# Chunks of both layers fetched row by row through SyncE, and a second range of layer 2's products placed at the end of layer 1

## The chip, the cores and the metric

The kernel runs on one core of one Trainium2 chip. The metric is the device time of one execution in microseconds (us), median of several runs. Engines are named as the profile names them: PE is TensorE (PEld its weight loads), DVE VectorE, ACT ScalarE, POOL GpSimd, SP SyncE; SPq is SyncE's stream of DMA issues.

## What is computed

Two layers of a graph network over 6250 nodes and 100000 edges, all in float32, then a residual and a layer norm. The edges are sorted by target node, and the targets are squared random numbers, so low nodes have many edges.

```python
def _gin_agg(h, src, dst, eps, n_nodes):
    agg = jax.ops.segment_sum(h[src], dst, num_segments=n_nodes)
    return (1.0 + eps) * h + agg
...
h = _gin_agg(x, src, dst, eps1, n)            # x: 6250 x 256
h = jax.nn.relu(h @ W1a + b1a)                # 256 -> 512
h = jax.nn.relu(h @ W1b + b1b)                # 512 -> 512
h = _gin_agg(h, src, dst, eps2, n)
h = jax.nn.relu(h @ W2a + b2a)                # 512 -> 512
out = h @ W2b + b2b                           # 512 -> 256
...
x = _layernorm(x + out)
```

## The kernel before

Nodes are taken in 49 tiles of 128, edges in 782 chunks of 128. The first 288 chunks belong to the seven lowest tiles, the heavy ones (`HEAVY`). They are not fetched at all: the kernel counts how often each source occurs for each heavy tile, and multiplies the matrix of counts with all node rows. In layer 1 that is `first_products`, over 13 ranges of four tiles (`RANGE`; the last range has one tile). The counts are written to DRAM (`counts`) and read back (`ci`, line 1557) for layer 2, where `second_products` splits each range's rows into two parts (`upper`, `xr`, lines 1532 to 1540) and makes 7 x 4 x 2 products for it (line 1644).

The other 494 chunks stand in 85 groups of 2 to 16 chunks, which are gone through from high nodes to low. For each chunk GpSimd fetches 128 rows by an indirect DMA (`gather`, line 507), from x in layer 1 (1 KB rows) and from h1 in layer 2 (2 KB rows). Four gathers make a piece, six pieces are in flight, in the buffers `early` and, in layer 2 only, `late` too. TensorE sums a chunk by a matmul with a selection matrix (`sums`, line 1172); `merge` moves the sums to their nodes (line 1235) and VectorE adds them to the accumulators (line 1245). When a block of tiles is complete, `dense` turns it over (line 1289), multiplies twice (lines 1342 and 1375) and stores h1, or the layer norm's result. Layer 2 goes first through two groups (`FORES`) that need little of the newest h1.

One chunk of some groups takes another way, in layer 1 only. `ferrying` loads its 128 row numbers into SyncE's registers, 16 at a time, and SyncE issues one transfer per row into `b2b_c`, a buffer that later holds a bias. The last matmul of the group reads `b2b_c` instead of the gather's buffer. Which groups these are is worked out beforehand (`ferries`, from the constants in `FERRY`): a group is chosen if 128 rows can be brought by the time its gathers have landed.

The order of instructions on every engine is fixed when the kernel is built. A planner (`Plan`) plays the whole layer through with assumed costs: processes ask for an engine, a buffer or a point in time, and each instruction is emitted when its request is granted. The assumed pitch of a gather is `GATHERS`, 1.28 us in layer 1 and 1.265 us in layer 2. An assumed time for a load to land (`LOAD`, `SEEDS`, `COUNTS`, `WHOLE`) only sets where the load's reader stands in its engine's order; on the chip the reader waits for the load itself. SyncE's issues cost nothing in the plan. On the chip each engine executes its own list in order and stops at the first instruction whose inputs or buffers are not ready.

`AHEAD2` says how many ranges of layer 2's products are placed in layer 1's order, at the lowest urgency (`first = 6`). Before, it is one: the last range, of one tile.

Of the kernel before, what the change touches and what calls it, by code (L numbers as in the profile page):

```python
# [10 lines left out]
F32 = mybir.dt.float32  # L11
I32 = mybir.dt.int32
# [5 lines left out]
P = 128  # L18
# [3 lines left out]
SLOTS = 32  # L22
# [25 lines left out]
PATIENT = 16.0  # L48
SOWN2 = 25.0
WEIGHT2 = 4.0  # L50
FERRY = (45.0, 14.0, 5.0, 16, 610.0)
LEAD = 1.5
LATE = (6, 8)
HASTE = -20.0
AHEAD2 = 1
ACCS2 = 4
AFTER = 4.0
ZEROS = 7
# [117 lines left out]
GATHERS = (1.28, 1.265)  # L176
# [181 lines left out]
def tile_gin_residual_layernorm(  # L358
# [106 lines left out]
    FORETOLD = range(min(lo[g] for g in FORES), max(hi[g] for g in FORES) + 1)  # L465
    orders = {1: list(reversed(range(BEGIN[0], NG)))}
    orders[2] = FORES + [g for g in reversed(range(BEGIN[1], NG)) if g not in FORES]
    ferries, t, free = [], FIRST, FERRY[0]
    for g in orders[1]:
        n = len(members[g])  # L470
        t += GATHERS[0] * n
        ready = free + FERRY[1] * P / FERRY[3] + FERRY[2]
        if ready <= t + LANDINGS[0] and t < FERRY[4] and members[g][-1][0] < full:
            ferries.append(g)
            t -= GATHERS[0]
            free = t + LANDINGS[0] + FERRY[2]
    pieces = {
        number: [
            (g, chunks[i : i + BURST])
            for g in order  # L480
            for chunks in [members[g][: -1 if number == 1 and g in ferries else None]]
            for i in range(0, len(chunks), BURST)
        ]
        for number, order in orders.items()
# [311 lines left out]
    def ordered(ctx):  # L796
# [42 lines left out]
        def layer(number, pools, table, width, scale, weights, ba, wide, at=None, aside=None, right=None):  # L839
# [299 lines left out]
            def sums():  # L1139
                size = 2 if once else 1  # L1140
                turns = [order[k : k + size] for k in range(0, len(order), size)]
                turn_of = {g: gs for gs in turns for g in gs}
                last = {g: i for i, (g, _) in enumerate(pieces[number])}
                final = next(i for i, (g, _) in enumerate(pieces[number]) if g in turns[-1])
                shared = {}
                i = 0
                while i < len(pieces[number]):
                    n = 1 if i >= final or (not once and pieces[2][i][0] in FORES) else min(
                        JOIN[number - 1], final - i
                    )  # L1150
                    some = range(i, i + n)
                    for i in some:
                        yield ("until", selected[pieces[number][i][0]])
                        yield ("until", arrived[i])
                        if once and i == last[pieces[1][i][0]] and pieces[1][i][0] in ferries:
                            yield ("until", ferried[pieces[1][i][0]])
                    for i in some:
                        gs = turn_of[pieces[number][i][0]]
                        if gs[0] not in shared:
                            shared[gs[0]] = yield ("get", banks, 0)  # L1160
                    yield ("on", "PE", TURN + SUMS * width * n, 0)
                    for i in some:
                        g = pieces[number][i][0]
                        gs = turn_of[g]
                        token = shared[gs[0]]
                        at = gs.index(g) * width
                        pm = bank[token.number][:, at : at + width]
                        sel, _, sel_token, _ = sels[g]
                        rows_, reads = gathered.pop(i)
                        for l, (c, b) in enumerate(pieces[number][i][1]):  # L1170
                            part = [c_ for c_, b_ in members[g] if b_ == b]
                            mm = nc.tensor.matmul(  # L1172
                                pm[b * SLOTS : (b + 1) * SLOTS],
                                sel[:, c - groups[g][0], :], rows_[:, l, :],
                                start=(c == part[0]),
                                stop=(c == part[-1] and (once or g not in FORES)),
                            )
                            if l == 0:
                                together(mm, reads[1:])
                        last_sum[i] = mm  # L1180
                        if once and i == last[g] and g in ferries:
                            c, b = members[g][-1]
                            part = [c_ for c_, b_ in members[g] if b_ == b]
                            nc.tensor.matmul(
                                pm[b * SLOTS : (b + 1) * SLOTS], sel[:, c - groups[g][0], :], b2b_c,
                                start=(c == part[0]), stop=True,
                            )
                            plan.then(landed[g].set)
                        if once:
                            begun_with["last_sum"] = mm  # L1190
                        fetch_rows(i + PIECES)
                        if i == last[g]:
                            sel_token.used()
# [889 lines left out]
            permits = Room(plan, SIDE, False)  # L2083
            if once:
                begun = [Event(plan) for _ in STEPS]
            def ferrying():
                yield ("rest", FERRY[0])
                n = FERRY[3]
                for g in ferries:
                    c = members[g][-1][0]  # L2090
                    for o in range(0, P, n):
                        _, rows_in = nc.values_load_multi_w_load_instructions(
                            src[c * P + o : c * P + o + n].rearrange("(a b) -> a b", a=1),
                            engines=[mybir.EngineType.SP], min_val=0, max_val=N - 1,
                            skip_runtime_bounds_check_because="an edge comes from a node",
                        )
                        for j, v in enumerate(rows_in):
                            nc.sync.dma_start(b2b_c[o + j : o + j + 1, :], x[bass.ds(v, 1), :])
                        yield ("rest", FERRY[1])
                    plan.at(plan.now + FERRY[2], ferried[g].set)  # L2100
                    yield ("until", landed[g])
                nc.sync.dma_start(b2b_c, b2b.partition_broadcast(P))

            ferried = {g: Event(plan) for g in ferries}
            landed = {g: Event(plan) for g in ferries}

            def fetching():
                yield ("rest", WEIGHTS if once else SOWN2 - plan.now)
# [4 lines left out]
                        yield ("rest", WEIGHT2)  # L2113

            plan.start(fetching())
            grouped = [b for b in range(len(blocks)) if any(uses[t] for t in blocks[b])]
            if once:
                for i in range(PIECES):
                    fetch_rows(i)
                plan.start(seeding(grouped, {}))  # L2120
                plan.start(seeding([b for b in range(len(blocks)) if b not in grouped], wanted))
                plan.start(selecting())
                plan.start(counting())
                plan.start(ferrying())
                first_products()
            else:
                second_products(list(reversed(range(len(ranges))))[AHEAD2:])
                begins = [b for b in grouped if blocks[b][0] >= tiles]
                plan.start(seeding([b for b in begins if blocks[b][0] not in FORETOLD], {}))
                plan.start(seeding_late([b for b in begins if blocks[b][0] in FORETOLD]))  # L2130
                for g in FORES:
                    plan.start(late_edges(g))
                plan.start(late_rows())
                plan.start(selecting())
                plan.ending = HASTE
                for i in range(PIECES):
                    fetch_rows(i)
# [37 lines left out]
    def general(ctx):  # L2175
# [8 lines left out]
        w2a_s, w2b_s, b2b_s, fetch = second(after)  # L2184
        for _ in fetch():
            pass
        acc1 = [gdram.tile([ROWS, D], F32, name=f"acc1_{k}") for k in range(NACC)]
        acc2 = [gdram.tile([ROWS, H], F32, name=f"acc2_{k}") for k in range(NACC)]

# [239 lines left out]
```

## Time and profile before

| | us |
|---|---|
| median of 3 runs | 1304.05 (1303.57 to 1305.85) |
| profiled execution, whole | 1301.3 |
| its span, first to last instruction | 1299.5 |
| TensorE busy | 1186.0 |
| GpSimd busy | 954.9 |
| VectorE busy | 877.5 |
| ScalarE busy | 621.5 |

Busy times are those of instructions; an indirect DMA keeps GpSimd busy while it writes the transfer's descriptors, and the 0.30 us between two of them count as idle. SyncE only issues transfers and loads registers, so it has no busy time here. The mean TensorE clock granted was 0.962 of full speed.

### The profile page before, as it was taken

How to read it: one execution, taken by the hardware profiler on the slowest of the kernel's cores; microseconds unless marked ns; L12 is line 12 of the kernel's file. 1: busy time of each engine (PE TensorE's matmuls, PEld its weight loads, DVE VectorE, ACT ScalarE, POOL GpSimd, SP SyncE). 2: the span in 40 equal slices, each digit the busy share in tenths (PEclk: the TensorE clock that was granted, in tenths of full speed). 3: DMA queues.
4: the chain of work that ended last, by engine and by line, in shares of the span. 5: the costliest groups of instructions: out<-in, count | busy, mean ns of one | idle time of the engine just before them, and what ended most of it. 6: DMA issues, size and time to landing. Idle time of an engine off the chain costs nothing.

```text
span 1299.5 us, 20725 instructions
## 1 busy us (share of the span) xinstructions
PE 1186.0 (91%) x6125; PEld 768.3 (59%) x6125; DVE 877.5 (68%) x2085; ACT 621.5 (48%) x1140; POOL 954.9 (73%) x997
## 2 busy tenths in 40 slices
PE   6879888889889989899788999899999999999987
PEld 4445455555455545455445677667776676766667
DVE  7997985878687979832156787678866665644334
ACT  6227766467646654674264453434343444432212
POOL 6777777777777777777777677777777777777770
PEclk9889999999999999899789899899999999999999
DMA  7446666567666665776599998898898899877771
GB/s 219 151 142 211 198 201 203 180 209 226 190 186 208 206 215 163 240 247 204 185 343 340 318 313 257 268 292 279 268 312 274 296 299 301 295 245 236 244 229 39
DMA packets 161978, 306.35 MB, mean 236 GB/s; under 512 B 26137, under 2 KB 94127, under 8 KB 161860
## 3 DMA queue, kind: packets, MB, share of 16 engines
q0 software_dynamic: 63040, 193.79, 47.9%
q1 hardware_dynamic: 77866, 86.72, 20.4%
q10 hardware_dynamic: 20954, 24.45, 5.4%
q8 instruction: 52, 0.85, 0.3%
q14 instruction: 66, 0.54, 0.1%
HBM read 274.42 MB, written 30.44 MB: 235 GB/s over the span
## 4 chain that ended last, share of the span: by engine, by line
PE 48%; DMA 17%; DVE 14%; ACT 8%; issue 6%; POOL 3%; SPq 2%; ACTq 1%; DVEq 1%; POOLq 0%
PE bank L1342 13%; PE bank L1375 10%; PE bank L1644 9%; PE bank L1172 7%; PE bank L1235 4%; DVE at L2074 3%; PE bank L1783 3%; DMA ci<-counts 3%; DMA late<-h,places 2%; DMA acc<-h 2%; DVE acc L1245 2%; DMA counts<-ci 2%; POOL early L507 2%; DVE cb L1857 2%; PE bank L1889 2%
## 5 line engine op out<-in xcount | busy, mean ns | idle before, releaser
L507 POOL DMA_INDIRECT early<-in_x_dram,srcs x490 | 481.5, 983 | 152.8 <-issue 132.0
L507 POOL DMA_INDIRECT early<-h,places x238 | 226.7, 953 | 75.4 <-issue 63.7
L507 POOL DMA_INDIRECT late<-h,places x232 | 221.9, 956 | 72.1 <-issue 57.3
L1245 DVE SCALAR_TENSOR_TENSOR acc<-bank,mask,acc 128x256 f32<-128x256 f32 (+1 forms) x360 | 205.1, 605 | 47.2 <-PE bank L1235 44.3
L1375 PE MATMUL bank<-w1b_s,ht 128*128 128x512 f32 (+1 forms) x392 | 188.8, 608 | 1.4 <-ACT ht L1352 0.8
L1342 PE MATMUL bank<-zt,w2a_s 128*128 128x256 f32 (+2 forms) x736 | 154.8, 364 | 0.2 <-ACT zt L1301 0.2
L1172 PE MATMUL bank<-early,sel 128*32 128x256 f32 (+1 forms) x1480 | 130.8, 468 | 24.1 <-DMA early<-h,places 8.5
L1644 PE MATMUL bank<-upper,cf 128*128 128x512 f32 (+1 forms) x343 | 148.8, 434 | 1.9 <-ACT upper L1532 1.1
L1342 PEld LDWEIGHTS bank<-zt,w2a_s 128*128 128x128 f32 x736 | 131.2, 193 | 24.1 <-issue 4.2
L1644 PE MATMUL bank<-xr,cf 128*128 128x512 f32 (+1 forms) x343 | 137.4, 401 | 1.1 <-DVE xr L1537 1.1
L2074 DVE TENSOR_TENSOR at<-bank,at 128x490 f32 x174 | 115.8, 666 | 28.3 <-ACT cf L1731 16.4
L1235 PE MATMUL bank<-split,to 128*128 128x256 f32 (+3 forms) x340 | 104.1, 426 | 18.8 <-DVE split L1226 6.9
L1026 DVE TENSOR_TENSOR sel<-iota,slot 128x256 f32<-128x256 f32 (+2 forms) x116 | 50.7, 437 | 98.4 <-PE bank L1172 95.0
L1375 PEld LDWEIGHTS bank<-w1b_s,ht 128*128 128x128 f32 (+1 forms) x392 | 74.2, 193 | 72.0 <-issue 60.7
L1342 PE MATMUL bank<-zt,w1a_s 128*128 128x256 f32 (+2 forms) x432 | 106.1, 397 | 9.4 <-ACT ht L1352 5.4
L1571 ACT CAST cf<-ci 128x512 fp32r<-128x512 uint16 (+1 forms) x91 | 54.1, 595 | 125.6 <-PE bank L1644 103.3
L1783 PE MATMUL bank<-xh,cf 128*128 128x512 f32 (+1 forms) x343 | 103.6, 438 | 9.3 <-DVE xh L1710 9.2
L1889 PE MATMUL bank<-cb,ca 128*128 128x490 f16 x288 | 86.0, 389 | 19.9 <-DVE at L2074 8.2
L1342 PEld LDWEIGHTS bank<-zt,w1a_s 128*128 128x128 f32 x432 | 84.2, 214 | 33.4 <-ACT ht L1352 6.3
L1172 PEld LDWEIGHTS bank<-early,sel 128*32 128x32 f32 x1480 | 40.2, 111 | 106.6 <-issue 62.5
L1710 DVE TENSOR_TENSOR xh<-bank,xh 128x512 fp32r<-128x512 f32 (+1 forms) x100 | 66.8, 672 | 43.1 <-ACT bank L1708 43.0
L1857 DVE TENSOR_SCALAR cb<-numbers,spot 128x490 f16<-128x490 f16 x288 | 90.7, 356 | 6.6 <-PE bank L1889 6.4
(193 smaller groups left out, 1764.0 us busy)
## 6 DMA issues: line engine op xcount, KB each, us to landing
raw<-in_x_dram SPq DMA_DIRECT2D x48, 512.0 KB
h<-h1r ACTq DMA_DIRECT2D x48, 256.0 KB
xr<-h SPq DMA_DIRECT2D x11, 1024.0 KB
counts<-ci ACTq DMA_DIRECT2D x84, 128.0 KB
ci<-counts SPq DMA_DIRECT2D x84, 128.0 KB
acc<-h SPq DMA_DIRECT2D x18, 512.0 KB
b2b_c<-in_x_dram SPq DMA_DIRECT2D x512, 1.0 KB
early<-in_x_dram,srcs POOLq DMA_INDIRECT x490
```

Source lines behind the costliest of these rows:

```text
L507: nc.gpsimd.indirect_dma_start(out=rows_[:, j, :], out_offset=None, in_=table, in_offset=bass.IndirectOffsetOnAxis(ap=rows_in[:, c - first ...
L1172: mm = nc.tensor.matmul(pm[b * SLOTS : (b + 1) * SLOTS], sel[:, c - groups[g][0], :], rows_[:, l, :], start=(c == part[0]), stop=(c == par ...
L1235: nc.tensor.matmul(pu[:, i * width : (i + 1) * width], to[:used], split[:used, l, :], start=(once or l == 0), stop=(once or l == 1),)
L1245: nc.vector.scalar_tensor_tensor(acc[t], pu[:, i * width : (i + 1) * width], mask[:, t - lo[g], g : g + 1], acc[t], op0=ALU.mult, op1=ALU.add,
L1342: nc.tensor.matmul(ph[:, (f - o) * TILES * P : (f - o) * TILES * P + nb], wa[:, k, f * P : (f + 1) * P], zt[:, k, :nb], start=(k == 0), st ...
L1375: nc.tensor.matmul(po[:m], ht[:, f, i * P : i * P + m], wb[:, f, :], start=(f == 0), stop=(f == KH - 1),)
L1644: nc.tensor.matmul(bank[token.number][:, :width], cf[:m, j, :], of[:m, j, :], start=(j == 0 and of is upper), stop=(j == len(ks) - 1 and o ...
L1710: begun_with["halves"] = nc.vector.tensor_tensor(xh[:m, two, 1, :], ap, xh[:m, two, 0, :], op=ALU.subtract)
L1783: nc.tensor.matmul(bank[tokens[i].number][:, : 2 * width], cf[:m, j, :], xh[:m, j, :, :].rearrange("p a d -> p (a d)"), start=(k == 0), st ...
L1857: made = nc.vector.tensor_scalar(token.tile, numbers, spot[:, c : c + 1], None, op0=ALU.is_equal)
L1889: mm = nc.tensor.matmul(bank[token.number][:, : NT * W], a.tile[:, c % BATCH, :], b.tile, start=(j == 0), stop=(j == n - 1),)
L2074: nc.vector.tensor_tensor(to, bank[token[0].number][:, : NT * W].rearrange("p (k w) -> p k w", w=W), to, op=ALU.add,)
```

## The change

More chunks take the row-by-row way, in both layers. In layer 1 batches hold 32 rows instead of 16. In layer 2 two buffers alternate: the first 512 columns of `srcs` and `dstf`, which layer 2 does not need any more; the row numbers are first written to a small table in DRAM (`rows2`). Both buffers are saved to DRAM at the end of layer 1 and restored in `general`, the branch for inputs that the main path can't handle. `AHEAD2` goes from 1 to 2, so that range 11 (four tiles) follows the last range in layer 1's order.

```diff
-FERRY = (45.0, 14.0, 5.0, 16, 610.0)
+FERRY = 32, 20.0, 5.0
+FERRY_FROM = (40.0, 5.0)
+FERRY_TO = (612.0, 596.0)
...
-AHEAD2 = 1
+AHEAD2 = 2
...
-    ferries, t, free = [], FIRST, FERRY[0]
-    for g in orders[1]:
-        n = len(members[g])
-        t += GATHERS[0] * n
-        ready = free + FERRY[1] * P / FERRY[3] + FERRY[2]
-        if ready <= t + LANDINGS[0] and t < FERRY[4] and members[g][-1][0] < full:
-            ferries.append(g)
-            t -= GATHERS[0]
-            free = t + LANDINGS[0] + FERRY[2]
+    ferries = {}
+    for number, order in orders.items():
+        ferries[number], free = [], [FERRY_FROM[number - 1]] * number
+        t, until = (FIRST, HASTE)[number - 1], FERRY_FROM[number - 1]
+        for g in order:
+            t += GATHERS[number - 1] * len(members[g])
+            ready = max(until, free[0]) + FERRY[1] * P / FERRY[0]
+            if (
+                ready + FERRY[2] <= t + LANDINGS[number - 1] and t < FERRY_TO[number - 1]
+                and members[g][-1][0] < full and not (number == 2 and g in FORES)
+            ):
+                ferries[number].append(g)
+                t -= GATHERS[number - 1]
+                until = ready
+                free = free[1:] + [t + LANDINGS[number - 1] + FERRY[2]]
+    rows2 = dram.tile([len(ferries[2]), P], I32, name="rows2")
+    lent = [
+        (t[:, :H], dram.tile([P, H], t.dtype, name=f"lent{i}")) for i, t in enumerate((srcs, dstf))
+    ]
...
-                        if once and i == last[pieces[1][i][0]] and pieces[1][i][0] in ferries:
-                            yield ("until", ferried[pieces[1][i][0]])
+                        if i == last[pieces[number][i][0]] and pieces[number][i][0] in ferried:
+                            yield ("until", ferried[pieces[number][i][0]])
...
-                                pm[b * SLOTS : (b + 1) * SLOTS], sel[:, c - groups[g][0], :], b2b_c,
+                                pm[b * SLOTS : (b + 1) * SLOTS], sel[:, c - groups[g][0], :], by_row[g],
...
+            by_row = [b2b_c] if once else [t.bitcast(F32) for t, _ in lent]
+            by_row = {g: by_row[i % len(by_row)] for i, g in enumerate(ferries[number])}
...
             def ferrying():
-                yield ("rest", FERRY[0])
-                n = FERRY[3]
-                for g in ferries:
-                    c = members[g][-1][0]
+                n = FERRY[0]
+                if not once:
+                    for i, g in enumerate(ferries[2]):
+                        c = members[g][-1][0] - NC2
+                        nc.sync.dma_start(
+                            rows2[i : i + 1, :].rearrange("a b -> b a"), places2[:, c : c + 1]
+                        )
+                yield ("rest", FERRY_FROM[number - 1] - plan.now)
+                for i, g in enumerate(ferries[number]):
+                    if i >= number:
+                        yield ("until", landed[ferries[number][i - number]])
+                    c = members[g][-1][0] * P
+                    listed = src[c : c + P].rearrange("(a b) -> a b", a=1) if once else rows2[i : i + 1, :]
                     for o in range(0, P, n):
                         _, rows_in = nc.values_load_multi_w_load_instructions(
-                            src[c * P + o : c * P + o + n].rearrange("(a b) -> a b", a=1),
-                            engines=[mybir.EngineType.SP], min_val=0, max_val=N - 1,
+                            listed[:, o : o + n], engines=[mybir.EngineType.SP],
+                            min_val=0, max_val=N - 1 if once else N,
...
                         for j, v in enumerate(rows_in):
-                            nc.sync.dma_start(b2b_c[o + j : o + j + 1, :], x[bass.ds(v, 1), :])
+                            nc.sync.dma_start(
+                                by_row[g][o + j : o + j + 1, :], table[bass.ds(v, 1), :]
+                            )
                         yield ("rest", FERRY[1])
                     plan.at(plan.now + FERRY[2], ferried[g].set)
-                    yield ("until", landed[g])
-                nc.sync.dma_start(b2b_c, b2b.partition_broadcast(P))
+                if once:
+                    yield ("until", landed[ferries[1][-1]])
+                    nc.sync.dma_start(b2b_c, b2b.partition_broadcast(P))
+                    for t, keeps in lent:
+                        yield ("rest", 8.0)
+                        nc.sync.dma_start(keeps, t)
```

## Rows read from the trace of the kernel before

**Rows 1.** Timeline of GpSimd: start, duration, instruction, idle before it and its releaser

```profile
636.13 0.94 POOL L507 DMA_INDIRECT early<-in_x_dram,srcs  x1 [0.30 <-issue]
638.39 0.94 POOL L507 DMA_INDIRECT early<-h,fore  x1 [1.32 <-issue]
...
1263.40 0.95 POOL L507 DMA_INDIRECT late<-h,places  x1 [0.30 <-DMA late<-h,places]
```

**Rows 2.** Gathers by tile: count, durations in ns, first and last start

```profile
L507 POOL DMA_INDIRECT early<-in_x_dram,srcs x490: 942/946/1614, 6.5 to 636.1; - x164
L507 POOL DMA_INDIRECT early<-h,places x238: 940/946/1211, 668.6 to 1258.4; - x119
...
L507 POOL DMA_INDIRECT late<-h,places x232: 942/946/1227, 681.2 to 1263.4; - x116
```

**Rows 3.** Waits of GpSimd from 640 to 1270 us: total, times, longest

```profile
POOL late L507 <- PE bank L1172: 3.2, 6, 1.7
POOL early L507 <- PE bank L1172: 3.2, 1, 3.2
```

**Rows 4.** Stretches: length, busy PE, PEld, DVE, ACT, POOL; clock, DMA share, GB/s

```profile
700.00:750.00 50.00, 43.41 (x220) 30.32 (x219) 35.00 (x60) 23.29 (x43) 35.84 (x38) 0.93 0.96 329
900.00:1000.00 100.00, 99.80 (x542) 71.47 (x541) 73.33 (x145) 43.68 (x80) 75.69 (x80) 1.00 0.88 289
```

**Rows 5.** Timeline of TensorE: sums that waited for gathers, and the end

```profile
639.09 1.08 PE L1172 MATMUL bank<-early,sel 128*32 128x256 f32 x8 [4.45 <-DMA early<-in_x_dram,srcs]
...
1253.55 1.30 PE L1172 MATMUL bank<-early,sel 128*32 128x512 f32 x8 [4.42 <-DMA early<-h,places]
...
1271.08 1.06 PE L1172 MATMUL bank<-late,sel 128*32 128x512 f32 x8
...
1290.73 1.89 PE L1375 MATMUL bank<-w2b_s,ht 128*128 128x256 f32 x8
```

**Rows 6.** SyncE's instructions of a row (L2098) and of a batch (L2092)

```profile
L2098 SPq FUSED_REGOPS  x512: 37/37/47, 19.4 to 532.7; - x171
L2098 SPq MOVE b2b_c<-in_x_dram x512: 29/29/38, 19.5 to 532.8; - x171
L2098 SPq DMA_DIRECT2D b2b_c<-in_x_dram x512: 224/228/309, 19.6 to 532.9; - x171
...
L2092 SPq TENSOR_LOAD <-in_src_dram_ptr x32: 1021/1936/3752, 15.6 to 520.4; - x32
...
L2092 SPq TENSOR_LOAD <-in_src_dram x32: 1724/1972/3207, 17.2 to 523.7; - x32
```

**Rows 7.** Timeline of SyncE's issues where the layers meet

```profile
595.72 3.69 SPq L1557 DMA_DIRECT2D ci<-counts  x2
640.25 0.93 SPq L1460 DMA_DIRECT2D xr<-h  x2
```

**Rows 8.** Waits of ScalarE, 40 to 560 us (two rows), 665 to 1260 us (one)

```profile
ACT xh L1701 <- DMA raw<-in_x_dram: 19.3, 6, 5.4
...
ACT acc L1002 <- DMA acc<-in_x_dram: 16.4, 5, 7.1
...
ACT acc L1002 <- DMA acc<-h: 17.2, 6, 5.9
```

**Rows 9.** Timelines of ScalarE and TensorE around one late seed

```profile
818.80 1.15 ACT L1002 ACTIVATE acc<-acc,e 128x1024 f32<-128x1024 f32 x1 [3.68 <-DMA acc<-h]
...
821.72 1.12 PE L1289 MATMUL bank<-ident,acc 128*128 128x128 f32 x4 [3.31 <-DVE xr L1537]
```

**Rows 10.** Timeline of TensorE: two products of layer 2 in a run

```profile
1207.82 0.39 PE L1644 MATMUL bank<-xr,cf 128*128 128x512 f32 x1
1208.05 0.39 PE L1644 MATMUL bank<-upper,cf 128*128 128x512 f32 x1
```

**Rows 11.** DMA queue of SyncE: packets, MB, share; whole span, then 130.3 to 147.3 us

```profile
q1 hardware_dynamic: 77866, 86.72, 20.4%
...
q1 hardware_dynamic: 79, 0.05, 1.0%
```

More of the change, by code (lines that the diff above doesn't have):

```diff
@@ L480, in tile_gin_residual_layernorm @@
             for g in order
-            for chunks in [members[g][: -1 if number == 1 and g in ferries else None]]
+            for chunks in [members[g][: -1 if g in ferries[number] else None]]
             for i in range(0, len(chunks), BURST)
@@ L1180, in sums @@
                         last_sum[i] = mm
-                        if once and i == last[g] and g in ferries:
+                        if i == last[g] and g in ferried:
                             c, b = members[g][-1]
@@ L2085, in layer @@
                 begun = [Event(plan) for _ in STEPS]
+            ferried = {g: Event(plan) for g in ferries[number]}
+            landed = {g: Event(plan) for g in ferries[number]}
+            by_row = [b2b_c] if once else [t.bitcast(F32) for t, _ in lent]
+            by_row = {g: by_row[i % len(by_row)] for i, g in enumerate(ferries[number])}
             def ferrying():
-                yield ("rest", FERRY[0])
-                n = FERRY[3]
-                for g in ferries:
-                    c = members[g][-1][0]
+                n = FERRY[0]
[11 more added lines that the diff above has]
+                    listed = src[c : c + P].rearrange("(a b) -> a b", a=1) if once else rows2[i : i + 1, :]
                     for o in range(0, P, n):
                         _, rows_in = nc.values_load_multi_w_load_instructions(
-                            src[c * P + o : c * P + o + n].rearrange("(a b) -> a b", a=1),
-                            engines=[mybir.EngineType.SP], min_val=0, max_val=N - 1,
+                            listed[:, o : o + n], engines=[mybir.EngineType.SP],
+                            min_val=0, max_val=N - 1 if once else N,
                             skip_runtime_bounds_check_because="an edge comes from a node",
@@ L2097, in ferrying @@
                         for j, v in enumerate(rows_in):
-                            nc.sync.dma_start(b2b_c[o + j : o + j + 1, :], x[bass.ds(v, 1), :])
+                            nc.sync.dma_start(
+                                by_row[g][o + j : o + j + 1, :], table[bass.ds(v, 1), :]
+                            )
                         yield ("rest", FERRY[1])
                     plan.at(plan.now + FERRY[2], ferried[g].set)
-                    yield ("until", landed[g])
-                nc.sync.dma_start(b2b_c, b2b.partition_broadcast(P))
-            ferried = {g: Event(plan) for g in ferries}
-            landed = {g: Event(plan) for g in ferries}
+                if once:
[4 more added lines that the diff above has]
+                        nc.sync.dma_start(keeps, t)
             def fetching():
@@ L2115, in layer @@
             plan.start(fetching())
+            plan.start(ferrying())
             grouped = [b for b in range(len(blocks)) if any(uses[t] for t in blocks[b])]
@@ L2123, in layer @@
                 plan.start(counting())
-                plan.start(ferrying())
                 first_products()
@@ L2186, in general @@
             pass
+        for t, keeps in lent:
+            nc.sync.dma_start(t, keeps)
         acc1 = [gdram.tile([ROWS, D], F32, name=f"acc1_{k}") for k in range(NACC)]
```

## Prediction

> **What bounds the kernel now.** I read the profile in this order: GpSimd's timeline, the gathers counted by tile, GpSimd's waits, the stretches by engine, TensorE's timeline where the layers meet and where the kernel ends, then SyncE's part.
>
> GpSimd's timeline comes first because it hardly has a hole. A gather is followed by the next one 1.25 us later (0.95 us of work, 0.30 us of issue), and from the last gather of layer 1 at 636.13 us to the first of layer 2 at 638.39 us little less than one gather is lost; the last starts at 1263.40 us [rows 1]. The gathers by tile give the counts: 490 in layer 1, 238 and 232 of layer 2 through the two buffers, and 12 more into each buffer for the two groups that go first [rows 2]. So layer 1's 490 take 6.5 to 637 us, 1.29 us each, and layer 2's 494 take 638.4 to 1264.4 us, 1.27 us each. The reader is to see that layer 2's run is paced by GpSimd itself: over its whole stretch it waits for the buffer's reader on TensorE for only 6.4 us [rows 3].
>
> Yet TensorE is nearly as full. From 900 to 1000 us it is busy 99.80 of 100 us; only from 700 to 750 us, where the DMA engines are 0.96 busy, does it have 6.6 us free [rows 4]. It stands still for want of a gather at two notable places: 4.45 us before layer 1's last sum and 4.42 us at 1253.55 us [rows 5]. After the last sum at 1271.08 us it has 21.5 us of work to 1292.6 us, and 6.9 us of closing steps follow it [rows 5]. So two clocks run side by side: GpSimd's count of gathers, and TensorE's work plus its stalls. Whichever is slower sets the end, and a gain on one counts only as far as the other can follow.
>
> The sum is made against the profiled execution: 1301.3 us, of which 1299.5 us are span. It lies 2.75 us under the median of 1304.05 us; I apply the change in span to the median.
>
> **The change: chunks brought row by row.** How many there are follows from the planner's lines. Before, a chunk takes 8 batches of 16 rows at 14 us plus 5 us, and the next one waits until the buffer has been used; ready times are 162, 283, 405 and 532 us: four chunks, which is the 512 row transfers of the trace [rows 6]. After, a chunk takes 4 batches of 32 rows at 20 us, from 40 us on: ready at 120, 210, 301, 392, 483 and 574 us, so six. In layer 2 two buffers alternate, so a chunk becomes ready every 80 us, from 85 to 565 us of the layer's own clock: seven. GpSimd therefore makes 9 gathers fewer, 2 in layer 1 and 7 in layer 2. At the pitch of 1.25 us that is 11.3 us; at the means of 1.29 and 1.27 us, 11.5 us. I take 11.3 us, because the excess over 1.25 us is not tied to single gathers. TensorE's share does not fall: each chunk still needs its product, only the source changes.
>
> **What SyncE pays.** A row costs 37 + 29 + 228 ns = 0.294 us of SyncE, and a batch two register loads of 1.94 and 1.97 us before it [rows 6]. A batch of 16 holds the queue for 8.6 us, one of 32 for 13.3 us, out of 20 us that the planner gives it. In layer 1 this is 24 batches, 319 us, in place of 32 batches, 275 us; in layer 2 it is new: 28 batches, 372 us. The copies of the row numbers out to DRAM (7 small transfers), the saving of two buffers and the load of the bias all lie near the layer's border, where SyncE has nothing to issue from 599.4 to 640.25 us [rows 7]; I cost them at nothing. Without that gap they would cost SyncE some ten issues of 0.3 to 0.5 us. The trace shows no transfer of 4-byte pieces out of a tile; from below it is nothing, from above the whole gap of 41 us could not be filled by seven.
>
> What is queued behind a batch matters more. SyncE issues in order, so a load of seeds (acc), of x (raw), of a range (xr) or of counts (ci) waits up to 13.3 us behind one, and ScalarE then waits for its landing, in order too. Layer 1 shows the price with batches of 8.6 us: ScalarE waits 19.3 us for raw and 16.4 us for acc. In layer 2, without batches, it waits 17.2 us for acc [rows 8]. Scaled by 13.3/8.6 = 1.55, layer 1's 35.7 us become 55, or 20 more; layer 2's acc waits, if they go to layer 1's 16.4 x 1.55 = 25, grow by 8. That is 28 us more on ScalarE, an estimate.
>
> How much reaches TensorE? One event can be followed: ScalarE waits 3.68 us for acc and TensorE 3.31 us three us later [rows 9], a share of 0.9. Of the 17.2 us in all, though, I find no second stop of that kind in the middle of layer 2, where TensorE is full [rows 4]; 3.31 of 17.2 is 0.19. The bounds are thus 28 x 0.19 = 5 us and 28 x 0.9 = 25 us of new stalls. I take 5 us, because TensorE usually has products queued that need none of this.
>
> **The second range.** 7 x 4 x 2 = 56 products of layer 2 move ahead of its start. In a run one begins 0.23 us after the other [rows 10], so 12.9 us of TensorE's work leave layer 2 and go to the end of layer 1. This is a move, not a saving: it pays as far as it fills time in which TensorE waits for gathers there, 4.45 us in the largest gap [rows 5]. ScalarE converts 7 counts and splits 4 tiles more in the same stretch, and SyncE loads the range (1 MB) and 0.9 MB of counts there rather than after 640 us. Taking 1.9 MB out of a stretch that moves 329 GB/s is up to 5.8 us of DMA time, and TensorE has 6.6 us of idling there [rows 4] that this could shorten. Bounds 0 and 5.8 us; I take 3 us. If the products come late instead, they stay in layer 2 at no loss against before.
>
> **Sum.** GpSimd's clock: -11.3 us. TensorE's clock: the two waits for gathers go, -4.45 - 4.42 = -8.9; the border, -3; new stalls, +5; together -6.9 us. The slower clock decides: about -7 us, so 1304.05 - 7 = 1297 us.
>
> **Rivals.**
> *GpSimd alone decides.* If the new stalls hide wholly and the border gives all of its 5.8 us, TensorE's clock moves by up to -14.7 us and the gathers decide: -11.3 us, 1293 us. For it: GpSimd has almost no waits on TensorE. Against it: TensorE has almost no slack. Were a fifth of the 21.5 us behind the last sum done earlier as well, it would be 1289 us.
>
> *SyncE's batches starve ScalarE* (the other side). The place is the loads of acc, raw and xr behind a 13.3 us batch; the price at a share of 0.9 is 25 us: -8.9 - 3 + 25 = +13 us, 1317 us. It turns slower when the stalls pass 11.9 us, a share of 0.43. For it: the followed event. Against it: batches of 8.6 us already hold SyncE for some 60% of layer 1 (8.6 of 14 us by the planner), and gathers keep their pace there.
>
> *The move is no gain.* If the products do not fit before layer 1's last tiles, and the stalls eat what is left, -8.9 + 8 leaves about -1 us, 1303 us. For it: the counts must be written out and read back before each product. Against it: by the code six of the seven tiles' counts come from earlier passes, and layer 1 makes this range's rows among its first.
>
> *One DMA engine takes all rows.* A stretch with 32 row transfers shows 79 packets on SyncE's queue, so a row is at most two packets and cannot be spread over 16 engines. The whole queue took 20.4% of 16 x 1299.5 us for 86.72 MB, 48.9 us per MB [rows 11]. Seven chunks of 128 rows of 2 KB are 1.84 MB, 90 us. Spread evenly this is 0.01 of the engines over the 560 us. On a single engine it is 0.16 on top of 0.88 [rows 4], so 1.04; the excess of 22 us would make gathers late by as much, and -11.3 + 22 gives +11 us, 1315 us. No row shows which engine moves a row. The Trainium skill speaks for this one (DMA: Bandwidth & Descriptors, section "Why a DMA increments its semaphore by 16 and not by 1"): a transfer from SyncE runs on a number of engines that divides its slowest dimension, and those are the lowest-numbered ones; by that rule a transfer on one engine always meets the same one. Layer 1's rows are half as long, at a lower load, so the gathers' even pace there neither confirms nor refutes it.
>
> **Chances.** The forecast 0.48 (its own range 1291 to 1301 us), GpSimd alone 0.20, the move is no gain 0.12, SyncE's batches 0.16, one engine 0.04. A change under 0.2%, 2.6 us, cannot be told from none here. Faster: 0.20 and all but 0.03 of the forecast, 0.65. Same: 0.12 + 0.03 = 0.15. Slower: 0.16 + 0.04 = 0.20. The range of 1289 to 1310 us takes in the full gain with the shorter end, and the batches' case up to half way to its full price; beyond it lie the rest of that case and the single engine.
>
> **What would show it.** Right: 488 gathers in layer 1 and 487 in layer 2; the pitch still 1.25 us; layer 1's last gather near 633.6 us and layer 2's last 7 to 11 us earlier; products of the second range between 600 and 660 us; ScalarE's waits for raw and acc near 55 and 25 us. Wrong: waits of TensorE for the row buffers; GpSimd waiting for TensorE by more than some 10 us; TensorE's idle time in layer 2 above 10 us per 100 us; waits for gathers that land later than before. If row transfers start behind waits on SyncE, the matmul of a brought chunk stops TensorE, which I cost at nothing since rows are due 5 us and more ahead of their use.

## The result, and the profile after

The change makes the kernel slower: 1645.3 us (1641.35 to 1650.02) in place of 1304.05, a ratio of 1.2615 with a 95% interval of 1.258 to 1.2651. The forecast was 1297 us with a range up to 1310. Ratios compare the fast runs of two kernels alone (those within 1.5% of a kernel's fastest), so that a ratio can differ a little from that of the medians.

The profiled execution took 1644.9 us, of which 1643.2 us are span: 343.7 us more than before. First the page of the changed kernel: busy time by engine (part 1), and the chain of work that ended last, by engine and by line (part 4).

```profile
PE 1245.9 (76%) x6125; PEld 801.3 (49%) x6125; DVE 876.6 (53%) x2085; ACT 619.0 (38%) x1140; POOL 942.5 (57%) x988
...
PE 37%; DMA 18%; SPq 18%; issue 9%; DVE 8%; ACT 7%; POOL 1%; ACTq 1%; DVEq 0%; POOLq 0%
SPq L2124 13%; PE bank L1387 9%; PE bank L1354 9%; PE bank L1184 5%; PE bank L1656 5%; SPq L2118 4%; DMA acc<-h 4%; DMA raw<-in_x_dram 3%; PE bank L1247 3%; PE bank L1795 3%; DVE acc L1257 2%; DMA sown<-h 2%; DMA acc<-in_x_dram 2%; PE bank L1901 1%; POOL early L519 1%
```

The same line of the kernel before:

```profile
PE 48%; DMA 17%; DVE 14%; ACT 8%; issue 6%; POOL 3%; SPq 2%; ACTq 1%; DVEq 1%; POOLq 0%
```

SPq is SyncE's queue of issues. Its share of the chain goes from 2% of 1299.5 us (26 us) to 18% of 1643.2 us (296 us), that of the DMAs from 221 to 296 us: 345 us together, about as much as the span has grown (the shares are whole per cent, so each of the four figures is good to some 8 us). The two lines named with SPq are the row transfers (L2124) and the register loads ahead of them (L2118).

The gathers by tile, as in [rows 2], then two stretches with the columns of [rows 4]:

```profile
L519 POOL DMA_INDIRECT early<-in_x_dram,srcs x488: 940/946/1715, 6.7 to 798.6; - x163
L519 POOL DMA_INDIRECT early<-h,places x235: 940/946/1967, 852.0 to 1601.7; - x118
L519 POOL DMA_INDIRECT early<-h,fore x12: 942/946/1104, 821.6 to 835.7; - x12
L519 POOL DMA_INDIRECT late<-h,places x228: 940/946/1535, 864.7 to 1606.7; - x114
```

```profile
300.00:400.00 100.00, 72.26 (x330) 43.09 (x331) 53.87 (x121) 50.02 (x86) 55.18 (x58) 0.85 0.51 155
900.00:1000.00 100.00, 70.88 (x341) 48.92 (x342) 55.69 (x101) 35.38 (x66) 53.00 (x55) 0.84 0.72 235
```

The counts are the forecast ones: 488, and 235 + 228 + 2 x 12 = 487 (the second buffer has its 12 too). But layer 1's last gather starts at 798.6 us and not at 636, and TensorE is busy for 70.88 us of the stretch from 900 us, where it was for 99.80 in the kernel before [rows 4]. No engine is full any more, and the DMA share has fallen from 0.88 to 0.72. The mean clock granted to TensorE in this stretch is 0.84 in place of 1.00. Over the whole span it is 0.872 in place of 0.962, and the same 6125 matmuls are busy for 1245.9 us in place of 1186.0. So the 343.7 us are 283.8 us of idle time more on TensorE (397.3 in place of 113.5) and 59.9 us of busy time more, at a lower clock.

Who waits? GpSimd, for TensorE to free its buffers, and ScalarE and VectorE, for loads that SyncE issues (total, times, longest; compare [rows 3] and [rows 8]):

```profile
POOL early L519 <- PE bank L1184: 271.1, 43, 21.6
POOL late L519 <- PE bank L1184: 79.9, 12, 17.8
...
ACT acc L1014 <- DMA acc<-h: 140.1, 14, 23.3
ACT xh L1713 <- DMA raw<-in_x_dram: 107.2, 11, 22.5
ACT acc L1014 <- DMA acc<-in_x_dram: 71.6, 8, 12.6
ACT upper L1544 <- DMA xr<-h: 41.3, 4, 13.3
...
DVE whole_acc L1634 <- DMA sown<-h: 43.7, 4, 22.9
DVE upper L1336 <- DMA upper<-in_x_dram: 40.7, 3, 19.7
```

VectorE's two rows in the kernel before:

```profile
DVE whole_acc L1622 <- DMA sown<-h: 9.8, 3, 6.2
DVE upper L1324 <- DMA upper<-in_x_dram: 9.0, 2, 7.2
```

ScalarE's four rows make 360 us in 37 waits, 9.7 us each; [rows 8] make 53 us in 17 waits, 3.1 us each. VectorE's two rows make 84 us in place of 19. TensorE does not wait for the rows themselves: the whole list of its waits has one for a row buffer, of 0.8 us. It is the other loads that come late. One event shows how the one becomes the other. The timelines of SyncE, ScalarE, TensorE and GpSimd around 330 us of the changed kernel; for a run of transfers SyncE's second column reaches from the first to the last:

```profile
316.72 16.44 SPq L2124 DMA_DIRECT2D b2b_c<-in_x_dram  x32
333.27 0.41 SPq L1472 DMA_DIRECT2D acc<-in_x_dram  x1
333.77 7.62 SPq L1472 DMA_DIRECT2D raw<-in_x_dram  x2
347.03 17.01 SPq L2124 DMA_DIRECT2D b2b_c<-in_x_dram  x32
...
336.06 0.72 ACT L1014 ACTIVATE acc<-acc,e 128x512 f32<-128x512 f32 x1 [11.58 <-DMA acc<-in_x_dram]
...
337.83 0.98 PE L1901 MATMUL bank<-cb,ca 128*128 128x490 f16 x2 [10.73 <-ACT split L1228]
...
335.36 0.95 POOL L519 DMA_INDIRECT early<-in_x_dram,srcs  x1 [0.30 <-issue]
347.51 0.94 POOL L519 DMA_INDIRECT early<-in_x_dram,srcs  x1 [11.19 <-PE bank L1184]
```

The load of the seeds (acc) comes out of SyncE as soon as the batch of 32 rows is through, at 333.27 us. ScalarE has waited for it for 11.58 us, TensorE for ScalarE for 10.73 us, GpSimd for TensorE for 11.19 us. All three engines lose the same eleven microseconds, one after the other.

Last, what a batch costs SyncE. The instructions of the register loads and of the rows (count, minimum, median and maximum in ns, first and last start), as in [rows 6]:

```profile
L2118 SPq TENSOR_LOAD <-rows x28: 3842/5998/9314, 836.4 to 1553.9; - x28
L2118 SPq TENSOR_LOAD <-in_src_dram_ptr x24: 1567/2162/3752, 15.9 to 713.6; - x24
...
L2118 SPq TENSOR_LOAD <-in_src_dram x24: 3334/3560/4468, 18.4 to 715.6; - x24
...
L2124 SPq FUSED_REGOPS  x1664: 37/37/51, 22.9 to 1572.9; - x185
...
L2124 SPq DMA_DIRECT2D srcs<-h x512: 224/228/307, 844.1 to 1573.0; - x171
```

The single instructions of a row last as long as before. The runs of them, in SyncE's timeline in layer 2, do not add up to their sum:

```profile
1104.76 13.41 SPq L2124 DMA_DIRECT2D srcs<-h  x32
1118.27 0.40 SPq L1472 DMA_DIRECT2D acc<-h  x1
...
1129.34 13.42 SPq L2124 DMA_DIRECT2D srcs<-h  x32
...
1149.80 13.04 SPq L2124 DMA_DIRECT2D srcs<-h  x32
```

13.41 us for 32 rows are 0.42 us a row, not 0.294; in layer 1, 16.44 us are 0.51. The step from one row to the next is 0.41 us in the median in both layers, 0.12 us more than the three instructions last; what makes the runs of layer 1 longer (13.0 to 18.4 us) is single stops in them, the longest of 3.8 us. A batch of layer 1 thus holds SyncE for 2.16 + 3.56 + 16.4 = 22 us and one of layer 2 for 6.0 + 13.4 = 19.4 us, where the planner gives 20 us to it and to everything else that SyncE loads. The 24 and 28 batches together come to some 1080 us, where the prediction had 319 + 372 = 691. The planned pace was not kept: by the first and last starts above, register loads begin every 30 us in layer 1 and every 27 us in layer 2.

### The profile page after: what moved, and what is told of

Read it like the earlier page. It is cut to its first block, busy times and chain, and to the rows that moved or that the text cites. A ratio compares the mean times of both kernels' runs of the same rounds, so it can differ in the third digit from the quotient of the medians.

```text
span 1643.2 us, 24226 instructions
## 1 busy us (share of the span) xinstructions
PE 1245.9 (76%) x6125; PEld 801.3 (49%) x6125; DVE 876.6 (53%) x2085; ACT 619.0 (38%) x1140; POOL 942.5 (57%) x988
## 4 chain that ended last, share of the span: by engine, by line
PE 37%; DMA 18%; SPq 18%; issue 9%; DVE 8%; ACT 7%; POOL 1%; ACTq 1%; DVEq 0%; POOLq 0%
SPq L2124 13%; PE bank L1387 9%; PE bank L1354 9%; PE bank L1184 5%; PE bank L1656 5%; SPq L2118 4%; DMA acc<-h 4%; DMA raw<-in_x_dram 3%; PE bank L1247 3%; PE bank L1795 3%; DVE acc L1257 2%; DMA sown<-h 2%; DMA acc<-in_x_dram 2%; PE bank L1901 1%; POOL early L519 1%
## 5 line engine op out<-in xcount | busy, mean ns | idle before, releaser
L519 POOL DMA_INDIRECT early<-in_x_dram,srcs x488 | 474.2, 972 | 322.6 <-PE bank L1184 171.2
L1387 PE MATMUL bank<-w1b_s,ht 128*128 128x512 f32 (+1 forms) x392 | 194.1, 625 | 25.2 <-ACT zt L1313 24.4
L1247 PE MATMUL bank<-split,to 128*128 128x256 f32 (+3 forms) x340 | 115.6, 461 | 122.8 <-ACT split L1236 60.7
L1184 PE MATMUL bank<-early,sel 128*32 128x256 f32 (+1 forms) x1470 | 137.9, 491 | 49.6 <-DVE at L2086 23.7
L1656 PE MATMUL bank<-upper,cf 128*128 128x512 f32 (+1 forms) x343 | 156.2, 455 | 12.1 <-DVE whole_acc L1601 9.6
L1795 PE MATMUL bank<-xh,cf 128*128 128x512 f32 (+1 forms) x343 | 110.6, 461 | 51.2 <-DVE xh L1722 51.2
L1247 PEld LDWEIGHTS bank<-split,to 128*128 128x128 f32 (+1 forms) x340 | 70.5, 216 | 160.1 <-ACT split L1236 63.9
L1387 PE MATMUL bank<-w2b_s,ht 128*128 128x256 f32 (+1 forms) x336 | 100.7, 430 | 47.4 <-ACT ht L1364 31.7
L1014 ACT ACTIVATE acc<-acc,e 128x512 f32<-128x512 f32 (+2 forms) x44 | 36.3, 842 | 212.2 <-DMA acc<-h 140.1
L1354 PE MATMUL bank<-zt,w1a_s 128*128 128x256 f32 (+2 forms) x432 | 105.4, 394 | 14.0 <-DVE at L2086 11.3
L1795 PEld LDWEIGHTS bank<-xh,cf 128*128 128x128 f32 (+1 forms) x343 | 70.3, 210 | 79.3 <-DVE xh L1722 58.4
```

Source lines behind the costliest of these rows:

```text
L519: nc.gpsimd.indirect_dma_start(out=rows_[:, j, :], out_offset=None, in_=table, in_offset=bass.IndirectOffsetOnAxis(ap=rows_in[:, c - first ...
L1184: mm = nc.tensor.matmul(pm[b * SLOTS : (b + 1) * SLOTS], sel[:, c - groups[g][0], :], rows_[:, l, :], start=(c == part[0]), stop=(c == par ...
L1247: nc.tensor.matmul(pu[:, i * width : (i + 1) * width], to[:used], split[:used, l, :], start=(once or l == 0), stop=(once or l == 1),)
L1354: nc.tensor.matmul(ph[:, (f - o) * TILES * P : (f - o) * TILES * P + nb], wa[:, k, f * P : (f + 1) * P], zt[:, k, :nb], start=(k == 0), st ...
L1387: nc.tensor.matmul(po[:m], ht[:, f, i * P : i * P + m], wb[:, f, :], start=(f == 0), stop=(f == KH - 1),)
L1656: nc.tensor.matmul(bank[token.number][:, :width], cf[:m, j, :], of[:m, j, :], start=(j == 0 and of is upper), stop=(j == len(ks) - 1 and o ...
```

## The experiments

Four theories stand against each other in the expectations. S: SyncE is full, so that every other load is late by a batch. T: the products of the second range, put ahead of layer 1's last steps, hold up the end of layer 1. U: the rows fill one DMA engine. B: one long batch ahead of an urgent load is enough, whatever share of SyncE's time the batches take. The expectations call some runs by number: e3 and e4 are the rows as changed in layer 1 and in layer 2 only, e5 is the quarter of the bytes, e6 half the pace in layer 2, e8 the fixed rows.

**Parts of the change.** Four kernels, compared with the kernel before at 1304.39 us (1295.95 to 1308.25) on the same chip.

*The second range alone*, in the kernel before:

```diff
-AHEAD2 = 1
+AHEAD2 = 2
```

> Only the second range moves (AHEAD2 = 2 in the kernel before); no chunk more is brought by rows. Theory S: the change is slow because SyncE is full. A batch of 32 rows with its register loads holds it for about 19.5 us of every 20 us, so every other load waits. By S this kernel has no added batch and lands near before, 1290 to 1310 us. Theory T: the second range's products block the end of layer 1; then this kernel takes 1400 us or more. Theory U: the rows all cross one DMA engine and delay the gathers; then this one is near before, as by S.

Measured: 1317.62 us, ratio 1.0108 (1.0033 to 1.0183). GpSimd's timeline of this run where the layers meet:

```profile
636.02 0.95 POOL L507 DMA_INDIRECT early<-in_x_dram,srcs  x1 [0.30 <-issue]
664.24 0.94 POOL L507 DMA_INDIRECT early<-h,fore  x1 [27.27 <-DMA ci<-counts]
```

Layer 1's last gather is where it was; layer 2's first one starts 25.9 us later than in [rows 1]. ScalarE's last store of h ahead of that gather stands at 656.26 us (635.19 in the kernel before), because TensorE comes to layer 1's last steps later. That is 21.1 of the 25.9 us; the row puts the end of the wait down to a load of counts, and the other 4.8 us are not traced. Part of it is regained by the end: the median is up by 13.2 us, 7.6 us above S's range and far under T's 1400 us. The products are not free at the border; they stand ahead of what layer 2 needs.

*The rows alone*, in the changed kernel:

```diff
-AHEAD2 = 2
+AHEAD2 = 1
```

> The rows of both layers as changed, but only one range of products at the end of layer 1. S and U: nothing comes back, 1620 to 1670 us. T: 1300 to 1400 us.

Measured: 1638.23 us, ratio 1.2575 (1.2505 to 1.2644). The rows make nearly all of the loss; beside them the second range costs the difference of the ratios, 0.004 or 5 us, within the two intervals.

*Rows as changed in layer 1 only* (no chunk by row in layer 2):

```diff
-FERRY_TO = (612.0, 596.0)
+FERRY_TO = (612.0, -100.0)
...
-AHEAD2 = 2
+AHEAD2 = 1
```

> Layer 1's six chunks in batches of 32 rows per 20 us, none in layer 2, one range. S: layer 1 stretches as in the changed kernel, whose last gather of layer 1 starts 162 us later, and layer 2 is as before: 1440 to 1480 us. U: rows of 1 KB at a DMA share of 0.5 to 0.6 are no load for one engine: under 1320 us. T: 1300 to 1320 us.

*Rows as changed in layer 2 only* (layer 1 keeps 16 rows in 14 us):

```diff
-FERRY = 32, 20.0, 5.0
-FERRY_FROM = (40.0, 5.0)
-FERRY_TO = (612.0, 596.0)
+FERRY = (16, 14.0, 5.0), (32, 20.0, 5.0)
+FERRY_FROM = (45.0, 5.0)
+FERRY_TO = (610.0, 596.0)
...
-AHEAD2 = 2
+AHEAD2 = 1
```

> Layer 1's four chunks at the old pace (16 rows per 14 us), seven chunks in layer 2 at the new one, one range. S: layer 1 as before, layer 2 longer by about 180 us: 1460 to 1510 us, with e3's excess over before adding up to the changed kernel's. U: most of the 341 us is here, over 1580 us. T: 1300 to 1320 us.

Measured: 1465.1 us for layer 1 (1.1258, 1.1196 to 1.1319) and 1488.7 us for layer 2 (1.1435, 1.1373 to 1.1496). The losses of 160.7 and 184.3 us sum to 345 us, against 341 us for the whole change: each layer pays for its own batches. ScalarE's waits follow. First two rows of the run with layer 1's rows, then three of the run with layer 2's:

```profile
ACT xh L1713 <- DMA raw<-in_x_dram: 102.7, 11, 17.1
...
ACT acc L1014 <- DMA acc<-in_x_dram: 73.2, 7, 13.1
```

```profile
ACT acc L1015 <- DMA acc<-h: 142.7, 14, 24.3
...
ACT upper L1545 <- DMA xr<-h: 43.4, 6, 14.5
...
ACT xh L1714 <- DMA raw<-in_x_dram: 25.1, 9, 4.7
```

Where layer 1 keeps its old batches, raw costs 25.1 us as it did before (22.0 over the whole span). The waits are tied to the batches of their own layer.

**Which property of the rows.** The kernels from here on ran on chips on which the kernel before itself takes 1658 to 1687 us and SyncE's register instructions, which last at most 0.05 us in the changed kernel's trace, reach 1.4 us (their median stays); each ratio is against the kernel before on the same chip, and forecasts in us do not apply.

*A quarter of each row's bytes*: the same transfers, the same register loads, one fourth of the data. It leaves out the rest of each row and clears the buffer once.

```diff
-                                by_row[g][o + j : o + j + 1, :], table[bass.ds(v, 1), :]
+                                by_row[g][o + j : o + j + 1, : width // 4],
+                                table[bass.ds(v, 1), : width // 4],
```

> The changed kernel, but each row transfer brings only the first quarter of a row (256 or 512 bytes); the rest of the row is left out, so the sums of the brought chunks lack it. S: SyncE is held as long as before, nothing comes back, 1600 to 1660 us. U (one DMA engine filled by the rows): a quarter of the bytes frees it, 1320 to 1420 us.

> The kernel of e5 again on another chip: the changed kernel with a quarter of each row's bytes (the rest is left out of the sums). S: 1600 to 1660 us. U: 1320 to 1420 us.

> The changed kernel with a quarter of each row's bytes (the rest is left out of the sums). S: 22 to 28% over the kernel before, as the changed kernel itself. U: under 8% over it.

Measured: 2062.24 us against 1661.22 in one run (1.24), then ratios of 1.251 (1.2378 to 1.2643) and 1.234 (1.2215 to 1.2465). With a fourth of the bytes the loss stays, and ScalarE's waits are there (third run: raw 148.1 us, acc from h 102.8, acc from x 99.8). Bytes on a single engine are not the cause: U falls.

*Fixed rows*: the row numbers are constants, so that the register loads and the register arithmetic go. It leaves out the lookup; batches, transfers and bytes stay.

```diff
-                        _, rows_in = nc.values_load_multi_w_load_instructions(
-                            listed[:, o : o + n], engines=[mybir.EngineType.SP],
...
+                        rows_in = range(o, o + n)
...
-                                by_row[g][o + j : o + j + 1, :], table[bass.ds(v, 1), :]
+                                by_row[g][o + j : o + j + 1, :], table[v : v + 1, :]
```

> The changed kernel without register loads: every chunk brings fixed rows (those of the same number as the partition), which leaves out the lookup of the row numbers. SyncE is then held about 13.4 of every 20 us, the share that the prediction assumed. S: most of the 341 us come back, 1320 to 1420 us, of which the second range's 14 us stay. B: the 13 us batches still starve the other loads, over 1500 us.

> The kernel of e8 again on another chip: the changed kernel with fixed row numbers in place of the register loads. S: 1320 to 1400 us, up to 7% over before, since SyncE is held 13.4 of 20 us. B: over 1500 us, 15% or more over before.

> [...] S: up to 7% over the kernel before on the same chip, SyncE being held about 13.4 of 20 us. B: 15% or more over it.

Measured: 1.0118 (1.008 to 1.0155), 1.0195 (1.0122 to 1.0268) and 1.0024 (0.9967 to 1.0081). SyncE's timeline and ScalarE's waits in the first run:

```profile
975.52 17.87 SPq L2120 DMA_DIRECT2D dstf<-h  x32
...
1005.22 9.72 SPq L2120 DMA_DIRECT2D dstf<-h  x32
```

```profile
ACT xh L1713 <- DMA raw<-in_x_dram: 37.5, 8, 16.0
...
ACT acc L1014 <- DMA acc<-in_x_dram: 22.8, 6, 6.1
...
ACT acc L1014 <- DMA acc<-h: 18.8, 3, 9.2
```

52 batches of 32 whole rows, at the same pace by the plan, cost 0 to 2% against the kernel before. But that kernel has 32 batches of its own with register loads, which cost 3 to 5% on these chips (below). Against the kernel without any rows on the same chip, by the quotient of the two ratios, fixed rows cost 7.0 and 4.6% (second and third run), and rows of a quarter of the bytes with their register loads 31 and 29%. So the register work makes about four fifths of the loss, and the batches that are left, with the second range, are not free. That speaks against U once more, with the same number of transfers and all bytes, and against B in its strong form. What the row transfers need of SyncE is what costs. Two things are not separated here: a fixed row is one instruction in place of three and needs no register load, and it is one of the same 128 neighbouring rows each time. Nor were fixed rows run on a chip like that of [rows 6].

*Half the pace in layer 2*, and *short batches at that pace*: layer 1 as before; in layer 2 three chunks, once 32 rows in 40 us, once 16 rows in 20 us.

```diff
+FERRY = (16, 14.0, 5.0), (32, 40.0, 5.0)
```

```diff
+FERRY = (16, 14.0, 5.0), (16, 20.0, 5.0)
```

> Layer 1's four chunks as before, layer 2 with 32 rows per 40 us in place of 20 (three chunks), one range. S: SyncE is held some 19.5 of 40 us and the other loads fit between, 1295 to 1325 us; three gathers fewer are worth at most 3.8 us. Theory B (it is the length of a batch, not the share of time): each load can still be 19.5 us late, and half of e4's excess of 184 us remains, 1380 to 1410 us.

> The kernel of e6 again on another chip: layer 1's four chunks as before, three chunks in layer 2 at 32 rows per 40 us, one range. S: 1295 to 1325 us, or up to 2% over the kernel before. B: half of e4's excess, 7% over before.

> Layer 1's four chunks as before, three chunks in layer 2 at 32 rows per 40 us, one range. S: within 2% of the kernel before on the same chip. B: 7% over it.

> As e6, the same three chunks, but in batches of 16 rows per 20 us: the share of SyncE is a little higher, the longest hold about half. S: within 1% of e6. B: clearly faster than e6, by 3% or more.

Measured: 1.065 (1.0597 to 1.0703), 1.0571 and 1.0605 for half the pace; 1.039 (1.0298 to 1.0483) for the short batches. A batch at half the pace, in the third run:

```profile
1174.36 28.39 SPq L2125 DMA_DIRECT2D dstf<-h  x32
...
1228.77 32.82 SPq L2125 DMA_DIRECT2D dstf<-h  x32
```

Half the pace lies far above S's 2% and near B's 7%. But the twelve runs of 32 rows of this trace hold SyncE for 16.0 to 33.0 us, 28 in the median, so half the pace did not free the queue as meant, and the three runs do not separate S from B. The pair gives a hint: equal rows in shorter batches are 2.4% faster by the ratios, where S had said at most 1% and B at least 3%, but the six runs of the short batches spread from 1715.12 to 1753.73 us, and their median of 1746.19 is 1.1% under the 1764.97 of half the pace on the same chip. ScalarE's wait for acc from h is 54.8 us in the one trace and 13.1 in the other. That the length of one hold is a part of the price, beside the share, is likely by this and not shown.

**Fewer rows than before.** *No chunk by row at all*, and *half the pace in layer 1*, both in the kernel before:

```diff
-FERRY = (45.0, 14.0, 5.0, 16, 610.0)
+FERRY = (45.0, 14.0, 5.0, 16, 0.0)
```

```diff
-FERRY = (45.0, 14.0, 5.0, 16, 610.0)
+FERRY = (45.0, 28.0, 5.0, 16, 610.0)
```

> The kernel before with no chunk brought by rows at all: GpSimd makes four gathers more, worth 5 us, and SyncE is free of batches, which hold it for about 10.5 of every 14 us of layer 1 before. S: the waits of ScalarE for raw and acc (35.7 us before) mostly go, and the time is within 1% of before, 1295 to 1312 us. B and U say the same; the run tells what layer 1's four chunks are worth now.

> The kernel before with no chunk brought by rows. S: within 1% of the kernel before where instructions come promptly; on the last chip, where every issue took longer, it was 4.7% faster.

> The kernel before without any chunk by rows, once more. S: where instructions come promptly, four gathers more cost 5 us and fewer late loads give part of it back: 1295 to 1312 us; on a slow chip 4 to 5% faster than before.

> The kernel before with 16 rows per 28 us in place of 14: two chunks by rows in layer 1 in place of four, so two gathers more (2.5 us), and SyncE held 12 of 28 us. S: between the kernel before and the one without rows; where instructions come promptly within 0.5% of before, on a slow chip 2 to 4% faster.

Measured without rows: 0.9529 (0.942 to 0.9638), 0.958 (0.9491 to 0.9669) and 0.966 (0.9607 to 0.9712). With two chunks at half the pace: 1589.81 us, 0.9587 (0.9534 to 0.9641), on the chip on which no rows took 1604.02. On these chips the four chunks of the kernel before were already too many, by more than the 1% that S allowed in the first run. Without them one wait of ScalarE for raw, acc or xr is left in the three lists, of 1.6 us. Two chunks at half the pace are 14 us better than none, not between as expected, though the two intervals still touch. The batches are not what makes these chips slow: without any rows the kernel still takes 1594.72 to 1620.5 us on them. Whether these versions gain on a chip that issues as promptly as that of [rows 6] was not seen; there the kernel before waits for 53 us [rows 8], so there may be less to win.

## Why the prediction was wrong

**The counts were right and did not matter.** 488 and 487 gathers, still 1.25 us apart where they run on; but 351 us of GpSimd's time now go into waits for TensorE, of which the forecast allowed some 10 before it would call itself wrong. A gain of 11.3 us on GpSimd's clock is nothing when the other clock is 344 us late.

**The step that failed first: what SyncE pays.** The prediction summed the durations of a row's three instructions, 0.294 us, and took the register loads from [rows 6] as if their length did not depend on the number of values. Measured: 0.42 us (layer 2) to 0.51 us (layer 1) a row over the runs shown, and 3.56 us for a load of 32 values, where 16 took 1.97; from the table that the kernel writes itself, 6.0 us. So 13.3 us of each 20 were in fact 19.4 to 22. The number was in the trace of before, one view further: the run of 16 rows, start to end, in SyncE's timeline.

```profile
52.98 6.51 SPq L2098 DMA_DIRECT2D b2b_c<-in_x_dram  x16
...
101.01 7.80 SPq L2098 DMA_DIRECT2D b2b_c<-in_x_dram  x16
```

0.41 and 0.49 us a row; 32 of them and the two loads of [rows 6] (3.9 us) make 17 to 20 us of the 20 that the plan gives, a queue with no slack. The old batches, by the same count, hold 10.4 to 11.7 of 14 us, not the 8.6 on which the prediction rested its case against the starved ScalarE.

**ScalarE's waits** were scaled by the length of a batch, 1.55 (28 us more); they grew by 307 us (360 - 53). There are 2.2 times as many of them, and each is 3.1 times as long. Why a hold that is about twice as long as before does that is argued and not shown: when the plan gives 20 us to 19.4 to 22 us of work, the next batch is due before the loads that the last one held back are out.

**The share that reaches TensorE** was taken at 0.19, with 0.9 as the upper bound. Measured, TensorE's idle time grew by 284 us, against 307 us of ScalarE's waits and 66 us of VectorE's (84 - 19) for loads of the same queue. That is a share of about 0.8, an estimate, since waits of two engines can overlap. It lies near the 0.9 of the event of [rows 9] and excludes 0.19; the "products queued that need none of this" did not carry TensorE through.

**The second range** was put at -3 us with no loss possible. Alone it costs 13.2 us (by the interval of its ratio, 4 to 24): the forecast looked for idle time of TensorE at the border and overlooked what stands behind the products in TensorE's order, the steps that end layer 1.

**The waits for gathers** that were to go (-8.9 us) count for nothing beside the others: TensorE waits 12.9 us for gathers in all, 16.2 before. **The clock** was no term of the sum: the same products are busy for 59.9 us more at the lower mean clock (0.872 in place of 0.962), 59.9 of the 343.7 us.

Among the rivals, "SyncE's batches starve ScalarE" (chance 0.16) named the place, the loads and the way of the wait, and gave 1317 us: its mechanism was right and its price too small by a factor of 26 (13 against 341 us), since it rested on the same 28 us. "One DMA engine takes all rows" is excluded as the cause by the rows of a quarter of the bytes and by the fixed rows, though no run shows which engine moves a row. "The move is no gain" was half right: the move is a loss, a small one beside the rest.

What is shown: the rows make the loss (the rows alone), each layer its own part (the rows of one layer), through SyncE's time for register loads and register-addressed issues (fixed rows, on the slower chips), not through bytes. Open: how much of it is the queue's share and how much the length of one hold, since the run meant to tell them apart met a slower issue; and why those chips issue later.

## What to carry to other kernels

Cost an in-order queue by the pitch of its runs, from first to last start, and not by the sum of instruction durations; then ask what share of the time it gets is left for the loads that queue behind. A queue without any busy time in the profile may still be the one that everything waits for, because issues do not count as busy time. Work moved ahead into an idle stretch is free only if nothing urgent stands behind it on its engine.

## What the runs showed of the hardware

A transfer of one row with its address in a register cost SyncE 0.41 us from start to start in the median, and 0.42 to 0.51 us over the runs shown, although its three instructions last 0.294 us; with a constant address 32 rows took 9.72 us in the quicker run shown, 0.30 us each. A register load took 1.97 us for 16 values and 3.56 us for 32, beside some 2 us for the pointer of an input; it took 6.0 us for 32 from a table that the kernel had written, in layer 2, where the DMA engines were busier too (0.72 against 0.51), and the two causes are not separated. And the same kernel took 1304 us on some chips and 1658 to 1687 us on others, where single register instructions of SyncE lasted up to 1.4 us, and there bringing chunks by row cost 3 to 5% even in the kernel before.
